# A graph network on one Trainium2 core: spreading rows in three bf16 parts instead of f32, with one table of places instead of two

## The chip, the cores and the metric

The kernel runs on 1 core of one Trainium2 chip. The metric is device time in microseconds (us) of one launch; lower is better. A "profiled execution" is one launch recorded instruction by instruction. Five engines work side by side, each through its own instructions in order, and wait for each other by semaphores: PE (TensorE, matrix products, with its weight loads shown apart as PEld), DVE (VectorE), ACT (ScalarE), POOL (GpSimd) and SP (SyncE, which here issues transfers).

## What is computed

There are N = 32768 nodes with rows of D = 256 numbers, and E = 524288 edges (`src`, `dst`), sorted by `dst`. Layer 0 is attention inside blocks of 128 nodes; layer 1 is a gated graph layer. Cut to what matters:

```python
h = relu(layernorm(x))
x = x + attention(h)                     # 256 blocks of 128 nodes, 8 heads of 32
h1 = relu(layernorm(x))
h = batchnorm(h1)
a_in  = segment_sum((h @ W_in  + b_in )[src] * iw[:, None], dst)
a_out = segment_sum((h @ W_out + b_out)[dst] * ow[:, None], src)
x = x + gate(concat(a_in, a_out), h)     # sigmoid and tanh gates
```

The sums are linear, so the kernel sums rows of `h1` first and multiplies by the weights afterwards. For `a_out` each edge needs the row `h1[dst]`, scaled by `ow`, and the results are to be added by `src`, in which the edges are not sorted.

## The kernel before

**Stages.** First the edges are counted and tables are made (to about 1035 us of the span). Then comes **spreading**, with the attention woven into it (1035 to 8983 us). It takes the edges in their `dst` order, builds for each one a message, which is its `h1[dst]` row times `ow`, and writes it to a place in HBM (`msg_d`) that groups the messages by blocks of `src`. Then the sums are made for both directions (8990 to about 15360 us), and the gates last.

**An item of spreading** is up to 128 edges whose `dst` lie in one block of 128 nodes. There are 4352 items in three phases, and a **round** is CI = 64 items. The functions `turns`, `fetch`, `spread_lanes`, `select`, `rank`, `product`, `place`, `scale` and `scatter` write the order out by hand under `manual_schedule`: turn t does step s of item t minus the lag of s, so each engine's instructions stand in the order of the turns, and within a turn in the order of the tuple `steps` (the product stands ahead of the place there).

- `fetch` (lag 0): SP loads the 128 rows of the block from `h1_d` into `hb`, 128 KB.
- `spread_lanes` (lag 4, every fourth item) and `select` (lag 6): PE spreads each edge's lane over the partitions (L1064), and DVE makes from it a 0/1 matrix `selT` in f32 (L1069) for four items at once. For each item DVE makes `oh`, a 0/1 matrix in bf16 that tells each edge's block of `src` among NB = 256 (L1071).
- `rank` (lag 8, PE, L1079) and `place` (lag 8, DVE, L1099): the table `R` in PSUM, 128 x 256 in f32, holds for each edge of the item and each block of `src` how many messages that block already has. `rank` adds products of `oh` to it, in bf16; `place` reads for each edge the one number that belongs to its block. There are **two tables**, and item i uses `R[i % 2]`. For each item three products are added to its table: all edges of item i-1 (`ones_b`), the rest of item i-2 (`triu`) and the earlier edges of item i (`tri`).
- `product` (lag 8, PE, L1075): `selT` times `hb` in f32 gives each edge its row (`mp`, two buffers). Each is two MATMUL records in the profile.
- `scale` (lag 9, ACT, L1091): times `ow`, into `msg`. `scatter` (lag 9, POOL, L1108): four indirect transfers at every fourth item, 128 messages each.

`rank` for item i+2 writes the table that `place` of item i reads, so it waits for that; `rank` for item i+1 does not.

**The attention** of one group of 512 nodes is a list of steps by turn (`group`): each is put with `@at(t)` into the turns of one round, after the turn's steps of spreading. 63 of the 64 groups lie in rounds of spreading, one in each; group 0 runs alone ahead. For each of a group's four blocks it makes scores (L837), their maxima (DVE, L845), the exponentials (ACT, L851), transposes (PE, L857), the products with V (L873), the output projection (L895), `x1g` (DVE, L899) and `h1g` (ACT, L922). Block b starts at turn B = 17 + 11 b. At turn B + 19 of the last block SP writes `h1g` to `h1_d`, from which later rounds fetch. Rounds stand in loop bodies of four (`UG`), and some of one.

**What sets the order** around the change is this hand-written list alone, on PE, DVE, ACT and SP; POOL follows its semaphores.

Of the kernel before, what the change touches and what calls it, by code (L numbers as in the profile page):

```python
# [23 lines left out]
KC = D // P  # L24
HC = H // KC
GB = 4
# [122 lines left out]
BF16 = mybir.dt.bfloat16  # L149
NB = 256  # L150
T1 = 128
# [348 lines left out]
def gnn_kernel(ctx, tc, x, src, dst, edge_attr, edge_type, w_in_e, w_out_e,  # L500
               Wq, bq, Wk, bk, Wv, bv, Wo, bo, gate_table, We, be,
               gamma, beta, W_in, b_in, W_out, b_out, W_x2i, b_x2i, W_h2h, out):
    nc = tc.nc
    N = x.shape[0]
# [4 lines left out]
    dram = ctx.enter_context(tc.tile_pool(name="dram", bufs=1, space=DRAM))  # L509


    cn = {}
# [30 lines left out]
    x1_d = dram.tile([N, D], F32, name="x1_d")  # L543
    h1T_d = dram.tile([D, N], F32, name="h1T_d")
    h1_d = dram.tile([N, D], F32, name="h1_d")
    rec_d = dram.tile([E + T2, 4], F32, name="rec_d")
    ends = [sum(PH[:k + 1]) for k in range(len(PH))]
    assert ends[-1] == E
# [11 lines left out]

    x1_g = x1_d.rearrange("(g b p) d -> g p b d", b=GB, p=P)
    h1_g = h1_d.rearrange("(g b p) d -> g p b d", b=GB, p=P)
    h1T_g = h1T_d.rearrange("(c p) (g n) -> g p c n", p=P, n=GN)


# [3 lines left out]
    soff = [before_each(nc, cpool, cn, t, f"src_off{k}") for k, t in enumerate(scnt)]  # L569
# [11 lines left out]
    for k, (lo, hi) in enumerate(edges):  # L581
        t = target_counts(nc, cpool, dcnt, doff, lo, hi, f"dcnt{k}")
        w0, node, r = item_tables(tc, cpool, cn, f"p{k}", t, lo, T1, CI, 0, NC1[k], hi, [("row", tab1_d[k][0:NC1[k]])])
# [55 lines left out]
    with tc.tile_pool(name="ld", bufs=1) as lp:  # L639
# [4 lines left out]
        for k in range(K):  # L644
            n, node = NC1[k], itp[k][1]
# [5 lines left out]
            r = lp.tile([CI, n], F32, name="r")  # L651
# [9 lines left out]
        g = lp.tile([P, 1], F32, name="g")  # L661
        nc.vector.tensor_copy(g, lead)
        for k in range(K):
            left = lp.tile([P, 1], F32, name="left")
            nc.vector.tensor_scalar(left, g, -1.0, float(NG), op0=ALU.mult, op1=ALU.add)
            at = lambda i: slice(i * K + k, i * K + k + 1)
# [20 lines left out]
    with ExitStack() as c1:  # L687
# [25 lines left out]
        xg, xb, x1g, h1g = (ap.tile([P, GB, D], F32, name=n) for n in ("xg", "xb", "x1g", "h1g"))  # L713
        hT, qT, h1T = (ap.tile([P, KC, GN], F32, name=n) for n in ("hT", "qT", "h1T"))
        nmr = ap.tile([P, GB], F32, name="nmr")

        mv, rstd = ([ap.tile([P, GB] + w, F32, name=f"{n}{i}") for i in range(2)] for n, w in (("mv", [2]), ("rstd", [])))

        def group(g, bias=None):
# [3 lines left out]
            def at(t):  # L723
                def put(f):
                    todo.setdefault(t, []).append(f)
                return put
# [100 lines left out]
            for b in range(GB):  # L827
# [89 lines left out]
                for n, u in enumerate(range(bs.start, bs.stop)):  # L917
                    h = {}

                    @at(B + 18 + n)  # L920
                    def _(u=u):
                        nc.scalar.activation(h1g[:, u], x1g[:, u], AF.Relu, bias=nmr[:, u:u + 1], scale=rstd[1][:, u:u + 1])  # L922

                    @at(B + 19 + n)
                    def _(u=u, h=h):
                        h["tp"] = transposed("pt" if u == 1 else "sc", h1g[:, u])

                    @at(B + 20 + n)
                    def _(u=u, h=h):
                        nc.scalar.copy(h1T[:, :, u * P:(u + 1) * P], h["tp"])  # L930
# [4 lines left out]

            @at(B + 19)
            def _():
                nc.sync.dma_start(h1_g[g], h1g)

            @at(B + 21)  # L940
            def _():
# [27 lines left out]
        ip = c1.enter_context(tc.tile_pool(name="p_i", bufs=NM))  # L969
        hp = c1.enter_context(tc.tile_pool(name="p_h", bufs=10))  # L970
        bp = c1.enter_context(tc.tile_pool(name="p_b", bufs=1, space=PSUM))
        pp = c1.enter_context(tc.tile_pool(name="p_ps", bufs=2, space=PSUM))
        p1 = c1.enter_context(tc.tile_pool(name="p_p1", bufs=1, space=PSUM))
        zm = fp.tile([P, T3 // P, MW], F32, name="zmsg")
        nc.vector.memset(zm, 0.0)
        nc.vector.memset(zm[:, :, FW:FW + 1], -1.0e6)
        eno = fp.tile([CI, T1], F32, name="eno")
        nc.gpsimd.iota(eno, pattern=[[1, T1]], base=0, channel_multiplier=0, allow_small_or_imprecise_dtypes=True)
        R = [p1.tile([P, NB], F32, name=f"R{i}") for i in range(2)]
        win = fp.tile([CI, T1 * 4], F32, name="win")  # L980
        wix = fp.tile([CI, 1], I32, name="wix")
        rown = fp.tile([1, CI], I32, name="rown")
# [9 lines left out]
        def spread(k, lo, hi):  # L992
# [6 lines left out]

            w0_1, node_1 = itp[k]  # L1000
            nc.scalar.dma_start(msg_d[k][hi - lo:hi - lo + T3].rearrange("(p e) w -> p e w", p=P), zm)
            for r in R:
                nc.tensor.matmul(r, cn["row0"], soff[k], start=True, stop=False, skip_group_check=True)

            def derive(c):

# [47 lines left out]
            def fetch(i, q, c, turn):  # L1054
                if q % 4 == 0:
                    c["at"] = numbers(c["row"][:, q:q + 4], [N - P] * 4)
                hb = turn["hb", i] = hp.tile([P, D], F32, name="hb")
                nc.sync.dma_start(hb, h1_d[ds(c["at"][q % 4], P)])

            def spread_lanes(i, q, c, turn):  # L1060
                if q % 4 == 0:
# [3 lines left out]

            def select(i, q, c, turn):
                if q % 4 == 0:
                    sel = turn["sel", i // 4] = sp.tile([P, 4, T1], F32, name="selT")
                    nc.vector.tensor_scalar(sel, turn["bc"], cn["lane"], None, op0=ALU.is_equal)  # L1069
                oh = turn["oh", i] = op.tile([P, NB], BF16, name="oh")  # L1070
                nc.vector.tensor_scalar(oh, cn["iota1"], c["ed"][:, 0, q:q + 1], None, op0=ALU.is_equal)  # L1071

            def product(i, q, c, turn):
                mp = turn["mp", i] = pp.tile([P, D], F32, name="mp")
                nc.tensor.matmul(mp, turn["sel", i // 4][:, q % 4], turn.pop(("hb", i)), start=True, stop=True)  # L1075

            def add(what, of, to, turn):
                oh = turn["oh", of]
                nc.tensor.matmul(R[to % 2], cn[what], oh, start=False, stop=False, skip_group_check=True)  # L1079

            def rank(i, q, c, turn):

                if i:
                    add("ones_b", i - 1, i, turn)
                if i > 1:
                    add("triu", i - 2, i, turn)
                add("tri", i, i, turn)

            def scale(i, q, c, turn):
                msg = msgs[i // 4 % NM]  # L1090
# [4 lines left out]
            def place(i, q, c, turn):  # L1095
                if q % 4 == 0:
                    c["pf"] = ip.tile([P, 4], F32, name="pf")
                jk = sp.tile([P, NB], F32, name="jk")
                nc.vector.scalar_tensor_tensor(jk, cn["iota1"], c["ed"][:, 0, q:q + 1], R[i % 2], op0=ALU.is_equal,  # L1099
                                               op1=ALU.mult, accum_out=c["pf"][:, q % 4:q % 4 + 1])  # L1100
                if q % 4 == 3:
                    c["pi"] = ip.tile([P, 4], I32, name="pi")
                    nc.vector.tensor_add(c["pi"], c["pf"], c["ed"][:, 3, q - 3:q + 1])
# [8 lines left out]
                        tc.add_to_no_dep_group(f"places{k}", s.ins)  # L1112


            steps = ((0, fetch), (4, spread_lanes), (6, select), (8, rank), (8, product), (8, place), (9, scale), (9, scatter))

            def turns(begin_at, end, nr, groups):

                with tc.For_i(begin_at, end, nr, hint_engines=ENGINES) as it:
                    cs, turn, todo, n = [], {}, {}, nr * CI  # L1120
                    last = steps[-1][0]
                    with tc.manual_schedule(engines=IN_ORDER):
                        for t in range(n + last):
                            r, q = divmod(t, CI)
                            if r < nr:
                                after = ds((it + (r + 1)).with_bounds(min_val=0, max_val=NC1[k]), 1)
                                if q == 0:
                                    cs.append({})
                                    begin(cs[r])
                                    if groups is not None:  # L1130
                                        for u, fs in group((it + groups + r).with_bounds(min_val=0, max_val=NG - 1)).items():
                                            assert u < CI + last
                                            todo.setdefault(t + u, []).extend(fs)
                                if q == 10:
                                    window(after)
                                if q == 24:
                                    more = derive(after)
                                if q >= 24:
                                    next(more, None)
                            for lag, step in steps:  # L1140
                                i = t - lag
                                if 0 <= i < n:
                                    step(i, i % CI, cs[i // CI], turn)
                            for f in todo.get(t, ()):
                                f()
                        add("ones_b", n - 1, n, turn)
                        add("triu", n - 2, n, turn)
                        add("triu", n - 1, n - 1, turn)

            window(slice(0, 1))  # L1150
            for _ in derive(slice(0, 1)):
# [272 lines left out]
```

## Time and profile before

| | |
|---|---|
| median of 11 runs | 17505.98 us (17489.43 to 17527.19) |
| profiled execution: its time, its span | 17473.85 us, 17472.0 us |
| mean granted TensorE clock | 0.913 |
| busy share of the span: PE, DVE, ACT, POOL | 81%, 58%, 38%, 53% |
| spreading with attention, 1100 to 8507 us: PE, DVE, ACT, POOL busy | 6174, 5115, 3607, 4145 of 7407 us |
| one round with attention, 2192.9 to 2305.0 us: the same | 98.1, 82.3, 58.2, 66.3 of 112.1 us |
| one round without attention, 8602 to 8700 us: the same | 59.7, 57.0, 32.3, 64.2 of 98.0 us |

The profiled execution is 32 us below the median of the runs. "Busy" for PE counts a matmul from its start to its modelled end; matmuls follow one another before the earlier one has ended, so the distance from start to start is what one costs. In a timeline, the first column is the start in us, the second the duration; `out<-in` are the tiles, and `[1.70 <-PE R L1079]` says that the engine sat idle for 1.70 us before and what it waited for. Line numbers are those of the kernel before.

### The profile page before, as it was taken

To read this page: it belongs to the slowest core of one execution; us is meant where nothing else is said; L and a number is where in the kernel's file an instruction comes from. 1 tells how busy PE (TensorE), PEld (TensorE's weight loads), DVE (VectorE), ACT (ScalarE), POOL (GpSimd) and SP (SyncE) were. 2 spreads that over 40 slices of the span, in tenths; PEclk is the share of its full clock that TensorE was granted. 3 is DMA by queue.
4 is the path that set the end of the run, shared out by engine and by line. 5 is a ranking of instruction groups with operands and counts; after the bars stand their busy time and mean duration, and the time that the engine had idled before them with its cause. 6 is when DMAs were issued, how large, how long until landed. Compare 5 with 4: busy or idle time off the path is not lost. (4 is left out here: it accounts for less than half of the span.)

```text
span 17472.0 us, 292322 instructions
## 1 busy us (share of the span) xinstructions
PE 14096.4 (81%) x71746; PEld 10263.3 (59%) x71746; DVE 10064.5 (58%) x33799; ACT 6700.4 (38%) x16865; POOL 9294.8 (53%) x9307
## 2 busy tenths in 40 slices
PE   2078888888888888888769889888888888888989
PEld 2045655555555555555457777777777777643433
DVE  8767667666766667667655555555555445422222
ACT  0034444444444444444334444444444444310000
POOL 0045555555555555555567667666666666621222
PEclk6589999999999899999889999999999999999999
DMA  1035555445555445555558888788878888843332
GB/s 63 10 123 169 163 164 166 158 154 163 168 159 162 158 134 164 160 162 163 165 174 241 229 232 236 220 227 223 231 218 228 220 225 230 195 126 106 115 115 90
DMA packets 1829631, 2975.49 MB, mean 170 GB/s; under 512 B 299499, under 2 KB 1288136, under 8 KB 1827671
## 3 DMA queue, kind: packets, MB, share of 16 engines
q1 hardware_dynamic: 1169398, 1550.90, 30.4%
q0 software_dynamic: 430768, 1160.40, 22.9%
q10 hardware_dynamic: 227888, 246.51, 4.6%
q8 instruction: 582, 9.54, 0.2%
q14 instruction: 995, 8.14, 0.2%
HBM read 2123.63 MB, written 1248.64 MB: 193 GB/s over the span
## 5 line engine op out<-in xcount | busy, mean ns | idle before, releaser
L1108 POOL DMA_INDIRECT msg_d<-msg,pi x4352 | 4288.3, 985 | 3018.6 <-ACT msg L1091 1069.2
L1230 POOL DMA_INDIRECT rows<-h_d,ixc x3584 | 3403.9, 950 | 1560.1 <-PE ps_i L1244 449.3
L1099 DVE SCALAR_TENSOR_TENSOR jk<-iota,edc,R 128x256 f32<-128x256 bf16 x4352 | 2076.1, 477 | 1896.2 <-PE R L1079 1867.2
L1091 ACT ACTIVATE msg<-mp,edc 128x256 f32<-128x256 f32 x4352 | 2056.8, 477 | 2738.4 <-PE mp L1075 2699.5
L1265 ACT ACTIVATE selo<-lane_row,sl 128x128 f32<-128x128 f32 x5040 | 1664.0, 391 | 3623.8 <-DVE sl L1262 2966.6
L1272 PE MATMUL ps_o<-m,selo 128*128 128x257 f32 x10080 | 2596.9, 395 | 336.4 <-ACT selo L1266 332.3
L1244 PE MATMUL ps_i<-rows,sel 128*128 128x257 f32 x8960 | 2511.8, 399 | 370.0 <-DVE acc L1248 295.0
L1075 PE MATMUL mp<-hb,selT 128*128 128x256 f32 x8704 | 2760.3, 401 | 8.1 <-ACT msg L1091 7.1
L1272 PEld LDWEIGHTS ps_o<-m,selo 128*128 128x128 f32 x10080 | 1876.7, 196 | 671.8 <-ACT selo L1266 261.5
L1244 PEld LDWEIGHTS ps_i<-rows,sel 128*128 128x128 f32 x8960 | 1572.5, 199 | 626.3 <-DVE acc L1248 402.2
L1237 DVE TENSOR_SCALAR sel<-lane_row,ed 128x128 f32<-128x128 f32 x4480 | 1394.1, 359 | 561.8 <-PE idle L1245 506.2
L1075 PEld LDWEIGHTS mp<-hb,selT 128*128 128x128 f32 x8704 | 1399.7, 202 | 82.6 <-ACT msg L1091 13.8
L1071 DVE TENSOR_SCALAR oh<-iota,edc 128x256 bf16<-128x256 bf16 x4352 | 1415.6, 325 | 4.1
L1079 PE MATMUL R<-oh,ones_b 128*128 128x256 bf16 x4352 | 1245.9, 286 | 119.5 <-DVE jk L1099 111.3
L1276 DVE SCALAR_TENSOR_TENSOR acc<-acc,blk,ps_o 128x257 f32<-128x257 f32 x1680 | 806.0, 480 | 826.7 <-PE ps_o L1272 630.6
L1079 PE MATMUL R<-oh,tri 128*128 128x256 bf16 x4352 | 1238.1, 284 | 0.0
L1079 PE MATMUL R<-oh,triu 128*128 128x256 bf16 x4352 | 1231.2, 283 | 0.0
L1248 DVE SCALAR_TENSOR_TENSOR acc<-acc,blk,ps_i 128x257 f32<-128x257 f32 x2240 | 1071.1, 478 | 252.1 <-DMA sin_d<-acc 137.4
L1262 DVE TENSOR_SCALAR sl<-m,blk 128x3 f32<-128x3 f32 x1680 | 426.8, 254 | 1363.6 <-DMA m<-msg_d 1354.1
L1230 POOL DMA_INDIRECT rows<-h_d,ixh x896 | 849.9, 948 | 385.2 <-issue 135.2
L1266 ACT ACTIVATE selo<-selo,one 128x384 f32<-128x384 f32 x1680 | 1031.4, 614 | 52.2
L1245 PE MATMUL idle<-lane_row,sel 128*128 128x128 f32 x4480 | 852.2, 279 | 148.3 <-DVE sel L1237 141.2
(366 smaller groups left out, 20238.5 us busy)
## 6 DMA issues: line engine op xcount, KB each, us to landing
m<-msg_d SPq DMA_DIRECT2D x1680, 396.0 KB
hb<-h_d SPq DMA_DIRECT2D x4352, 128.0 KB
sin_d<-acc SPq DMA_DIRECT2D x2240, 128.5 KB
sout_d<-acc SPq DMA_DIRECT2D x1680, 128.5 KB
msg_d<-msg,pi POOLq DMA_INDIRECT x4352
more<-sout_d ACTq DMA_DIRECT2D x128, 514.0 KB
rows<-h_d,ixc POOLq DMA_INDIRECT x3584
a<-sin_d ACTq DMA_DIRECT2D x64, 514.0 KB
```

Of the source, the lines that this page charges most:

```text
L1071: nc.vector.tensor_scalar(oh, cn["iota1"], c["ed"][:, 0, q:q + 1], None, op0=ALU.is_equal)
L1075: nc.tensor.matmul(mp, turn["sel", i // 4][:, q % 4], turn.pop(("hb", i)), start=True, stop=True)
L1079: nc.tensor.matmul(R[to % 2], cn[what], oh, start=False, stop=False, skip_group_check=True)
L1091: nc.scalar.activation(msg[:, q % 4, 0:D], turn.pop(("mp", i)), AF.Copy, scale=c["ed"][:, 1, q:q + 1])
L1099: nc.vector.scalar_tensor_tensor(jk, cn["iota1"], c["ed"][:, 0, q:q + 1], R[i % 2], op0=ALU.is_equal, op1=ALU.mult, accum_out=c["pf"][:, q ...
L1108: s = nc.gpsimd.indirect_dma_start(out=msg_d[k][:], out_offset=bass.IndirectOffsetOnAxis(ap=c["pi"][:, j:j + 1], axis=0), in_=msgs[i // 4 ...
L1230: nc.gpsimd.indirect_dma_start(out=rows[(2 * i + r) % NR][:, 0:D], out_offset=None, in_=h1_d[:], in_offset=bass.IndirectOffsetOnAxis(ap=(i ...
L1237: nc.vector.tensor_scalar(sel[:, r], cn["lane_row"], c["ed"][:, 0, r, i:i + 1], c["ed"][:, 1, r, i:i + 1], op0=ALU.is_equal, op1=ALU.mult)
L1244: nc.tensor.matmul(ps, sel[:, r], rows[(2 * i + r) % NR], start=(r == 0), stop=(r == 1))
L1248: nc.vector.scalar_tensor_tensor(acc[0][i % NA], acc[0][(i - 1) % NA], c["blk"][:, 0, i:i + 1], c.pop(("t_ps", i)), op0=ALU.mult, op1=ALU.add)
L1265: nc.scalar.activation(sel[:, r], cn["lane_row"], AF.Abs, bias=sl[:, r:r + 1])
L1272: nc.tensor.matmul(ps, sel[:, r], m[:, r, 0:FW], start=(r == 0), stop=(r == T3 // P - 1))
```

## The change

`group` now writes the rows of `h1` a second time, to `h1s_d`, as three bf16 parts whose sum is the row: the row rounded to bf16, what is left rounded again, and what is left then. These are two ACT copies and two DVE subtractions for each block of 128 nodes. The write of `h1s` (768 KB for each group, at turn B + 22) takes SP; the write of `h1g` moves from SP to ACT. `fetch` loads the three parts (192 KB for each item). `selT` becomes bf16, and `product` is three bf16 matmuls into one `mp`, which gets a third buffer. `rank` keeps one table `R` and adds two products for each item, the rest of item i-1 and the earlier edges of item i. `place` stands ahead of `product` in the tuple.

```diff
+    h1s_d = dram.tile([N, 3, D], BF16, name="h1s_d")
...
+        h1s = ap.tile([P, GB, 3, D], BF16, name="h1s")
+        rest = ap.tile([P, GB, D], F32, name="rest")
...
+                    @at(B + 19 + n)
+                    def _(u=u):
+                        nc.scalar.copy(h1s[:, u, 0], h1g[:, u])
+
+                    @at(B + 20 + n)
+                    def _(u=u):
+                        nc.vector.tensor_sub(rest[:, u], h1g[:, u], h1s[:, u, 0])
+                        nc.scalar.copy(h1s[:, u, 1], rest[:, u])
+
+                    @at(B + 21 + n)
+                    def _(u=u):
+                        nc.vector.tensor_sub(h1s[:, u, 2], rest[:, u], h1s[:, u, 1])
...
             @at(B + 19)
             def _():
-                nc.sync.dma_start(h1_g[g], h1g)
+                nc.scalar.dma_start(h1_g[g], h1g)
+
+            @at(B + 22)
+            def _():
+                nc.sync.dma_start(h1s_g[g], h1s)
...
-        pp = c1.enter_context(tc.tile_pool(name="p_ps", bufs=2, space=PSUM))
+        pp = c1.enter_context(tc.tile_pool(name="p_ps", bufs=3, space=PSUM))
...
-        R = [p1.tile([P, NB], F32, name=f"R{i}") for i in range(2)]
+        R = p1.tile([P, NB], F32, name="R")
...
-                hb = turn["hb", i] = hp.tile([P, D], F32, name="hb")
-                nc.sync.dma_start(hb, h1_d[ds(c["at"][q % 4], P)])
+                hb = turn["hb", i] = hp.tile([P, 3, D], BF16, name="hb")
+                nc.sync.dma_start(hb, h1s_d[ds(c["at"][q % 4], P)])
...
-                    sel = turn["sel", i // 4] = sp.tile([P, 4, T1], F32, name="selT")
+                    sel = turn["sel", i // 4] = sp.tile([P, 4, T1], BF16, name="selT")
...
                 mp = turn["mp", i] = pp.tile([P, D], F32, name="mp")
-                nc.tensor.matmul(mp, turn["sel", i // 4][:, q % 4], turn.pop(("hb", i)), start=True, stop=True)
-
-            def add(what, of, to, turn):
-                oh = turn["oh", of]
-                nc.tensor.matmul(R[to % 2], cn[what], oh, start=False, stop=False, skip_group_check=True)
+                hb = turn.pop(("hb", i))
+                for part in range(3):
+                    nc.tensor.matmul(mp, turn["sel", i // 4][:, q % 4], hb[:, part], start=(part == 0), stop=(part == 2))
+
+            def add(what, of, turn):
+                nc.tensor.matmul(R, cn[what], turn["oh", of], start=False, stop=False, skip_group_check=True)
 
             def rank(i, q, c, turn):
 
                 if i:
-                    add("ones_b", i - 1, i, turn)
-                if i > 1:
-                    add("triu", i - 2, i, turn)
-                add("tri", i, i, turn)
+                    add("triu", i - 1, turn)
+                add("tri", i, turn)
...
-                nc.vector.scalar_tensor_tensor(jk, cn["iota1"], c["ed"][:, 0, q:q + 1], R[i % 2], op0=ALU.is_equal,
+                nc.vector.scalar_tensor_tensor(jk, cn["iota1"], c["ed"][:, 0, q:q + 1], R, op0=ALU.is_equal,
...
-            steps = ((0, fetch), (4, spread_lanes), (6, select), (8, rank), (8, product), (8, place), (9, scale), (9, scatter))
+            steps = ((0, fetch), (4, spread_lanes), (6, select), (8, rank), (8, place), (8, product), (9, scale), (9, scatter))
...
-                        add("ones_b", n - 1, n, turn)
-                        add("triu", n - 2, n, turn)
-                        add("triu", n - 1, n - 1, turn)
+                        add("triu", n - 1, turn)
```

More of the change, by code (lines that the diff above doesn't have):

```diff
@@ L562, in gnn_kernel @@
     h1_g = h1_d.rearrange("(g b p) d -> g p b d", b=GB, p=P)
+    h1s_g = h1s_d.rearrange("(g b p) s d -> g p b s d", b=GB, p=P)
     h1T_g = h1T_d.rearrange("(c p) (g n) -> g p c n", p=P, n=GN)
@@ L1001, in spread @@
             nc.scalar.dma_start(msg_d[k][hi - lo:hi - lo + T3].rearrange("(p e) w -> p e w", p=P), zm)
-            for r in R:
-                nc.tensor.matmul(r, cn["row0"], soff[k], start=True, stop=False, skip_group_check=True)
+            nc.tensor.matmul(R, cn["row0"], soff[k], start=True, stop=False, skip_group_check=True)
             def derive(c):
```

## The prediction

> **What bounds the kernel now.** I read the page's slices first, then busy time by stage, then the waits of spreading, and last the timeline of a few turns, because the change trades work on one engine for an order between two. The slices are 437 us each, in tenths:
>
> ```profile
> PE   2078888888888888888769889888888888888989
> ...
> DVE  8767667666766667667655555555555445422222
> ```
>
> Slices 4 to 20 are spreading. PE is busiest but never full there, and DVE is close behind. By stage (all spreading with attention, one round with attention, one without; columns are PE, PEld, DVE, ACT, POOL busy us, granted clock, DMA share, GB/s):
>
> ```profile
> 1100.00:8507.00 7407.00, 6174.24 (x35713) 4337.28 (x35711) 5115.37 (x18694) 3607.36 (x9306) 4144.78 (x4125) 0.92 0.50 161
> ...
> 2192.90:2305.00 112.10, 98.12 (x574) 68.85 (x572) 82.33 (x300) 58.21 (x151) 66.28 (x66) 0.94 0.54 172
> ...
> 8602.00:8700.00 98.00, 59.67 (x388) 42.48 (x388) 57.03 (x243) 32.30 (x82) 64.22 (x65) 0.80 0.53 172
> ```
>
> In a round with attention neither PE nor DVE fills the 112.1 us; together they do, by turns. In the round without attention nothing but POOL does: a scatter starts every 1.29 us, so 64 take 82.6 us, and the rest is start and drain. Who waits in the woven stage, and what ended DVE's waits ahead of `place` in the one round:
>
> ```profile
> ACT msg L1091 <- PE mp L1075: 2398.3, 2256, 5.1
> DVE jk L1099 <- PE R L1079: 1828.7, 1933, 4.7
> ...
> PEld pt L857 <- ACT pr L851: 262.9, 126, 2.3
> ```
> ```profile
>   PE R L1079: 27.8, 30
> ```
>
> DVE waits for the table in 30 of 64 items: there PE paces. In the other 34 DVE comes to `place` late, after its attention work, and PE runs ahead. Four turns of both, items 36 to 39 of one round:
>
> ```profile
> 2966.18 0.28 PE L1079 MATMUL R<-oh,ones_b 128*128 128x256 bf16 x1
> ...
> 2966.72 0.48 DVE L1099 SCALAR_TENSOR_TENSOR jk<-iota,edc,R 128x256 f32<-128x256 bf16 x1 [1.70 <-PE R L1079]
> ...
> 2966.95 0.27 PE L1079 MATMUL R<-oh,ones_b 128*128 128x256 bf16 x1
> ...
> 2967.13 0.42 DVE L899 TENSOR_TENSOR x1g<-mm,xb 128x256 f32<-128x256 f32 x1
> ...
> 2967.72 0.27 PE L1079 MATMUL R<-oh,ones_b 128*128 128x256 bf16 x1
> ...
> 2968.14 0.66 DVE L845 TENSOR_REDUCE nm<-sc 128x4 f32<-128x512 f32 x1
> ...
> 2968.91 0.47 DVE L1099 SCALAR_TENSOR_TENSOR jk<-iota,edc,R 128x256 f32<-128x256 bf16 x1
> ...
> 2969.31 0.69 DVE L865 COPY PT<-pt 128x512 f32<-128x512 f32 x1
> ...
> 2970.15 0.41 PE L857 MATMUL pt<-ident,pr 128*128 128x128 f32 x2 [1.50 <-ACT pr L851]
> ...
> 2970.39 0.27 PE L1079 MATMUL R<-oh,ones_b 128*128 128x256 bf16 x1
> ...
> 2970.77 0.47 DVE L1099 SCALAR_TENSOR_TENSOR jk<-iota,edc,R 128x256 f32<-128x256 bf16 x1
> ```
>
> `rank` of items 36, 37, 38, 39 starts at 2966.18, 2966.95, 2967.72, 2970.39; their places at 2966.72, 2968.91, 2970.77. PE begins rank 38 1.2 us before place 37 begins. Two tables allow that; one does not.
>
> **The change, part by part.** All per round with attention (63 of them), then times 63.
>
> *PE work.* From rank to rank with nothing between is 0.77 us (2966.95 to 2967.72): three bf16 products at 0.11, and the f32 product in two records for the remaining 0.43. The new item is two and three bf16 products, 5 x 0.11 = 0.55. That is 0.21 us less for each item, 13.7 a round, 930 us of PE time in all. The weight loads (L1079, three an item today) lie beside the products now; I take it that the three loads of `selT` do too. In the 34 items where DVE paces nothing of it shows; in the 30 where PE does, at most 30 x 0.21 = 6.4 us a round.
>
> *The order between rank and place.* New chain of each item: rank start to place start 0.42 (0.11, then 0.27 of the second product, then 0.04; today with three 0.54), place 0.48, about 0.07 to PE: 0.97 us an item at least, and rank i+1 behind place i. I walked items 30 to 41 of this round (one attention block) through the timeline with today's durations, each engine in its order. From item 36, with its rank left at 2966.18: place 36 ends 2967.08, rank 37 goes to 2967.15 (+0.20). DVE's L899 to L845 and `oh` then run 0.12 earlier than today, place 37 ends 2969.27, so rank 38 goes to 2969.34 (+1.62). The transposes of L857 wait for the copy of L865 anyway, so they start at 2970.03, before today's. Place 38 follows L865, the `selT` of four items (0.74) and `oh`: 2970.65 to 2971.13, rank 39 at 2971.20 (+0.81). Rank 40 comes at 2972.30 (+0.50), rank 41 at 2973.27 (+0.71). Over the whole block, with the 0.21 taken off each item, rank 41 is 0.97 us later than today, which is 17.11 us after rank 30. Three such blocks in a round: **+3.0**; the last, shorter stretch I take at half a block, **+0.5**. The eleven items at the round's start with 512-column products, where PE paces clearly, get the full saving: **-2.4**.
>
> *The parts of h1.* Eight DVE subtractions; `x1g` (L899, 128x256 f32) takes 0.42, about 0.34 in a row with others, so 2.7 us. They fall at turns 59 to 62 and 70 to 71, where DVE is mostly the later one: two thirds on the path, **+1.8**. Eight ACT copies, between L889 (0.38, from PSUM) and L922 (0.62, from SBUF): 4 us beside 58 of 112 busy, at zero, hidden by PE and DVE; the copies wait for a subtraction of the same turn, and behind them stand `scale` and the exponentials. The third `mp` lets PE go on then. Without that cover it is the whole 4.
>
> *Queues.* The write of `h1s` (768 KB) waits on SP for the last subtraction and for all fetches under way, and the next fetches stand behind it. Today, in one round, fetching stops at 2179.96, the 512 KB write goes at 2186.84 and the next fetch at 2190.43, a hole of 10.5 us; a fetch is used eight turns later, 14 us. With 1.5 times the bytes the hole is 12.3: still covered, at zero; past 14 it is paid in full. At a body's end POOL is last: in the body that ends near 2420 the write goes at 2410.66, POOL's last scatter ends at 2419.92 and fetching resumes at 2425.61. A write three turns later that takes 5.4 us is inside that. The write of `h1g` costs ACT 0.4 (L942's issue, 0.38), at zero. Bytes: 64 KB more for 4352 fetches and 768 KB for 64 groups, 335 MB over 7950 us, 42 GB/s on 161; the sums stage runs at 225. Zero. The rounds without attention stay at POOL's 1.29, since 0.97 is below it. All later stages read `h1_d` as before: zero.
>
> *The clock.* Where PE is busy 98.12 of 112.1, the granted clock is 0.94; at 59.67 of 98.0 it is 0.80. Taking 13.7 us out of about 115 makes PE 73% busy, which lies at 0.86 on the line between the two rows. That is 8% of PE's pace: 9 us a round if PE paced all of it, nothing where DVE does. The row without attention holds a long start and drain, so the woven row is nearer; I take **+1.5** and keep 0 to 9.
>
> [...]
>
> *Sum:* 3.0 + 0.5 - 2.4 + 1.8 + 1.5 = **+4.4 us a round**, times 63 = **+277 us**, on the profiled execution's 17473.85: 17,751. That execution is 32 us under the median of the runs; on the median, 17,505.98 + 277, it is **17,783 us**, 1.6% slower.
>
> **The rivals.**
>
> *PE paces, the wait is absorbed (faster).* If rank's later start falls into waits that PE has anyway, as at L857 above (1.50 idle), the saving is 30 x 0.21 less the subtractions: -6.4 + 1.8 = -4.6 a round, -290 us: 17,216. For it: DVE's 1828.7 us of waiting for R, and 0.12 less from rank to place. Against it: the walk, in which +1.62 came down only to +0.71, because PE-heavy turns follow DVE-heavy ones, and one table turns the sum of both into the sum of the larger.
>
> *The lag is paid in full (much slower).* In the round of the walk 26 of 64 places end after the next rank has started; the largest of each run, added up, are 16 us. With 1.8 and 5 for the clock, less 2.4, that is +20 a round, +1,290: 18,796. Against it: L857 shows that part of each lag meets a wait.
>
> *They cancel.* -2.4 and -1.0 against 3.0 and 0.5 with subtractions hidden: within 35 us of 17,506.
>
> *The bf16 parts save nothing.* If three loads of the same weights do not hide, each product costs up to 3 x (0.11 + 0.10) = 0.63 instead of 0.43. The load of L1079 takes 0.10 and shows no cost in the 0.11 steps, so I give it little: with +0.2 in 30 items, +6 more on the sum, +655 in all: 18,161.
>
> **How the numbers follow.** The sum's own case 0.62, with own range +1 to +9 a round (the clock from 0 to 9, the stretches walked only in part): 17,570 to 18,075. PE paces: 0.22. Cancel: 0.06. Paid in full: 0.06. Parts save nothing: 0.04. What a measurement of this kernel can tell from no change is about 0.2%, 35 us. The range for 8 in 10 reaches to the upper half of the faster case and to the rival with the unhidden loads: 17,300 to 18,150. Faster over 0.2%: 0.23, the first rival and a rest of the sum's low end. Within: 0.06. Slower: 0.71.
>
> **What would show it.** In the new profile: the line of the product with 13,056 matmuls that follow at 0.11; the table with two products an item; DVE waiting for R in more items but for less in each; PE waiting for DVE's `jk`, which today is near nothing, for several us in each round; PE less busy and clock under 0.92 from 1100 to 8507; a round of about 116 us; unchanged rounds without attention and unchanged later stages. Wrong would be: rounds near 107 with little waiting for `jk` (the first rival), a round far above 120 (the lag, or the clock), or PE waiting for `hb` (the queue).

## The result, and the profile after

| | before | after |
|---|---|---|
| median of the runs | 17,503.89 us (31 runs) | 17,931.14 us (17,902.98 to 17,942.44, 8 runs) |
| ratio, 95% interval | | 1.0242 [1.0233, 1.0251] |
| profiled execution: time, span | 17,473.85, 17,472.0 us | 17,956.11, 17,954.4 us |
| mean granted clock | 0.913 | 0.881 |

The change costs 2.4%. The forecast was 17,783 us, in a range of 17,300 to 18,150. The direction was right; the size was 148 us short. The two profiled executions lie further apart than the medians, 482 us against 427, so the loss that is taken apart below from the profiles is some 55 us larger than the loss in the table.

All of it is lost in spreading. From the first `place` to the last it takes 7,919.0 us before and 8,403.6 us after, +484.6; the two profiled executions differ by 482.3. In the slices of the new page the loss is seen as a lower clock over the first half; the last line is the clock of the page before:

```profile
PE   2077777777777768777758888888888888889888
...
PEclk6578888888888888888889999999999999999999
```
```profile
PEclk6589999999999899999889999999999999999999
```

By stage, the same stretch of the span as before, 1100 to 8507 us (PE, PEld, DVE, ACT, POOL busy, granted clock, DMA share, GB/s):

```profile
1100.00:8507.00 7407.00, 5678.22 (x33679) 3852.45 (x33678) 4998.42 (x18102) 3557.87 (x9246) 3938.04 (x3886) 0.84 0.61 191
```

PE did 496 us less here (6174.24 to 5678.22) and POOL got less far, 3,886 instructions against 4,125. No engine became fuller: DVE, ACT and POOL all fell too. So no engine became the bound; waiting grew. Who waits, 1100 to 8950 us (us in all, times, longest):

```profile
ACT msg L1111 <- PE mp L1098: 2329.1, 2007, 4.7
DVE jk L1119 <- PE R L1101: 2106.0, 2147, 4.2
...
PE R L1101 <- DVE jk L1119: 928.5, 1098, 4.0
...
ACT h1s L940 <- DVE rest L939: 376.1, 249, 2.7
...
PEld pt L743 <- ACT PT L867: 188.1, 62, 3.1
```

The same view of before:

```profile
DVE jk L1099 <- PE R L1079: 1846.6, 1961, 4.7
...
PE R L1079 <- DVE jk L1099: 111.3, 73, 3.3
...
PEld pt L739 <- ACT PT L863: 40.7, 63, 1.4
```

Three things are new. PE waits for `place` before it may change the one table: 111 us became 929. (What such waits cost is another question: e3 below has 1,020 us of them and is faster than after.) ACT waits 376 us for the first subtraction: 249 waits, one for nearly every block of the 63 groups. And PE's transposes of L743 wait longer for ACT's copy of `PT`, although no step of the change touches that copy.

To see where in a round the time goes, I took the distances from `place` to `place` in the 28 rounds that have attention and no end of a loop body near, and added them in three stretches. The busy times and the clock are those of the same stretches. The other columns are the first four experiments below, which ran on a chip where before takes 17,520 us.

| mean of 28 rounds, us | before | after | e1 two tables | e2 one table alone | e3 no parts made | e4 filler |
|---|---|---|---|---|---|---|
| whole round | 112.95 | 121.49 | 116.8 | 113.6 | 114.9 | 121.3 |
| items 0 to 47 | 82.86 | 86.75 | 81.10 | 84.41 | 84.95 | 86.90 |
| their clock | 0.97 | 0.91 | 0.96 | 0.98 | 0.94 | 0.99 |
| items 48 to 55 | 13.35 | 18.57 | 19.58 | 12.76 | 14.35 | 18.12 |
| their DVE, ACT busy | 8.7, 9.3 | 10.8, 11.1 | 10.8, 11.0 | 8.6, 9.3 | 8.7, 9.1 | 10.7, 11.2 |
| their clock | 0.88 | 0.62 | 0.64 | 1.00 | 0.72 | 0.78 |
| items 56 to 63 | 16.74 | 16.17 | 16.13 | 16.46 | 15.60 | 16.31 |

Eight items, 48 to 55, take 5.2 of the 8.5 us that a round lost. These are the turns in which the parts of `h1` are made. The windows of one round show the same stretch, before and then after:

```profile
3097.80:3111.10 13.30, 11.13 (x71) 8.32 (x72) 8.76 (x38) 9.31 (x24) 5.98 (x7) 0.87 0.37 122
```
```profile
3251.60:3269.90 18.30, 14.85 (x75) 10.71 (x75) 10.81 (x43) 11.10 (x30) 7.32 (x9) 0.63 0.41 124
```

DVE does 2.05 us more and ACT 1.79 us more, but the stretch is 5.0 us longer, and neither is full: DVE is busy 10.8 of 18.3 us, where it was 8.8 of 13.3. A turn of it, in the timeline of after (start, duration, engine):

```profile
3255.90 0.27 PE L1101 MATMUL R<-oh,triu 128*128 128x256 bf16 x1
...
3256.01 0.27 PE L1101 MATMUL R<-oh,tri 128*128 128x256 bf16 x1
...
3256.32 0.48 DVE L1119 SCALAR_TENSOR_TENSOR jk<-iota,edc,R 128x256 f32<-128x256 bf16 x1 [1.02 <-PE R L1101]
...
3256.92 0.42 DVE L939 TENSOR_TENSOR rest<-h1g,h1s 128x256 f32<-128x256 f32 x1
...
3257.37 0.40 ACT L940 CAST h1s<-rest 128x256 bf16<-128x256 f32 x1 [0.77 <-DVE rest L939]
...
3258.76 0.57 ACT L867 COPY PT<-pt 128x512 f32<-128x512 f32 x1
...
3259.38 0.69 PE L743 MATMUL pt<-ident,h1g 128*128 128x128 f32 x2 [2.77 <-ACT PT L867]
...
3260.53 0.40 PE L1101 MATMUL R<-oh,triu 128*128 128x256 bf16 x1
...
3260.72 0.42 PE L1101 MATMUL R<-oh,tri 128*128 128x256 bf16 x1
...
3261.18 0.48 DVE L1119 SCALAR_TENSOR_TENSOR jk<-iota,edc,R 128x256 f32<-128x256 bf16 x1 [3.65 <-PE R L1101]
...
3261.93 0.42 DVE L939 TENSOR_TENSOR rest<-h1g,h1s 128x256 f32<-128x256 f32 x1
...
3262.38 0.41 ACT L940 CAST h1s<-rest 128x256 bf16<-128x256 f32 x1 [2.68 <-DVE rest L939]
```

Read it as a ring. `place` (DVE) ends at 3256.80, and the subtraction stands behind it. ACT has waited 0.77 us for the subtraction of this same turn. Behind that cast on ACT stand the copy of `h1T`, the next cast, `h1g`, and the copy of `PT` (3258.76 to 3259.33). PE's transposes wait for `PT`, 2.77 us idle, and `rank` of the next item stands behind the transposes in PE's order. So the next `place` starts at 3261.18, 4.86 us after this one, and DVE has waited 3.65 of them. Each turn passes through all three engines one after the other, once for each cast.

### The profile page after: what moved, and what is told of

The parts are those of the page before. It is cut to its first block, busy times and chain, and to the rows that moved or that the text cites. A ratio compares the mean times of both kernels' runs of the same rounds, so it can differ in the third digit from the quotient of the medians.

```text
span 17954.4 us, 289429 instructions
## 1 busy us (share of the span) xinstructions
PE 13900.9 (77%) x71740; PEld 9969.0 (56%) x71740; DVE 10255.1 (57%) x34311; ACT 6870.6 (38%) x17377; POOL 9344.4 (52%) x9307
## 5 line engine op out<-in xcount | busy, mean ns | idle before, releaser
L1098 PE MATMUL mp<-hb,selT 128*128 128x256 bf16 x13056 | 2478.0, 305 | 3.8 <-DMA hb<-h1s_d 3.3
L1101 PE MATMUL R<-oh,triu 128*128 128x256 bf16 x4352 | 1308.2, 301 | 1029.3 <-DVE jk L1119 1016.1
L1098 PEld LDWEIGHTS <-selT 128*128 128x128 bf16 x13056 | 1422.4, 109 | 311.4 <-issue 5.6
L1092 DVE TENSOR_SCALAR oh<-iota,edc 128x256 bf16<-128x256 bf16 x4352 | 1367.2, 314 | 4.1
L1101 PEld LDWEIGHTS <-tri 128*128 128x128 bf16 x4352 | 448.8, 103 | 1619.1 <-issue 1582.9
L1101 PE MATMUL R<-oh,tri 128*128 128x256 bf16 x4352 | 1327.4, 305 | 0.0
```

The source lines that it names most:

```text
L1098: nc.tensor.matmul(mp, turn["sel", i // 4][:, q % 4], hb[:, part], start=(part == 0), stop=(part == 2))
L1101: nc.tensor.matmul(R, cn[what], turn["oh", of], start=False, stop=False, skip_group_check=True)
```

## The experiments

"After" is the changed kernel. The theory at the start: two costs, the order of one table and the making of the parts, with the lower clock as a consequence. The rivals: the clock itself costs the time; the larger transfers do.

### e1: two tables again

```diff
-        R = p1.tile([P, NB], F32, name="R")
+        R = [p1.tile([P, NB], F32, name=f"R{i}") for i in range(2)]
...
-        pp = c1.enter_context(tc.tile_pool(name="p_ps", bufs=3, space=PSUM))
+        pp = c1.enter_context(tc.tile_pool(name="p_ps", bufs=2, space=PSUM))
...
-                    add("triu", i - 1, turn)
-                add("tri", i, turn)
+                    add("ones_b", i - 1, i, turn)
+                if i > 1:
+                    add("triu", i - 2, i, turn)
+                add("tri", i, i, turn)
...
```

The third `mp` is given up for the second table: `mp` has two buffers here.

> The changed kernel with its tables undone: two tables R in turn, three products an item for them, and two mp buffers as before (the bank of the third goes to the second table). Rows stay in three bf16 parts. If the wait of rank for the place just ahead is the main cost (theory A), PE's waits for jk go from 928 us to about the 109 of before, and the time from 17,931 to about 17,580 (63 rounds less 3.5 for the order and about 2 of clock). If the lower clock is the main cost (B), PE's work rises only by 0.11 of the missing 0.21 us an item and about half of the loss comes back: about 17,720. If making or moving the parts is (C), it stays above 17,850.

Measured: 17,736.78 us, 1.0128 [1.0111, 1.0145], 194 us under after. The time is near the 17,720 of theory B, but what is seen inside is theory A: PE's waits for `jk` fall from 928.5 to 140.2 us, while the clock of 1100 to 8950 us rises only from 0.84 to 0.86. A's 17,580 isn't reached, since the cost of the parts stays. In the table above, items 0 to 47 fall from 86.75 to 81.10 us, below before's 82.86: there the bf16 products do save, 1.8 us, as long as the places alternate between tables. Items 48 to 55 stay long (19.58). So on top of bf16 rows one table costs 5.65 us in items 0 to 47 and 4.7 over the whole of such a round, and the trouble of the parts doesn't come from it.

### e2: one table alone

```diff
-        R = [p1.tile([P, NB], F32, name=f"R{i}") for i in range(2)]
+        R = p1.tile([P, NB], F32, name="R")
...
-                    add("ones_b", i - 1, i, turn)
-                if i > 1:
-                    add("triu", i - 2, i, turn)
-                add("tri", i, i, turn)
+                    add("triu", i - 1, turn)
+                add("tri", i, turn)
...
```

This and e10 start from the kernel before; all others from after.

> The kernel before with one table alone: two products an item for R, rows and product in f32, two mp buffers. A: the wait alone costs about what it costs in the change, 3.5 to 7 us a round, less up to 0.11 in the items that PE paces: 17,504 rises to about 17,750, with several hundred us of PE waiting for jk. B: half of the missing PE work, so half of the loss, 17,700, and a clock near 0.88 from 1100 us to the end of spreading. C: no loss, 17,500 or below.

Measured: 17,569.15 us, 1.0028 [1.0016, 1.0041]. That is below what either theory A (17,750) or B (17,700) expected. PE waits 747.6 us for `jk` here, and the loss, net of the table product that each item saves, is 49 us. The clock of 1100 to 8950 us is 0.93, not the 0.88 of B. The same table costs 49 us here and 194 us in e1's comparison. With f32 rows items 0 to 47 lose 1.55 us, and items 48 to 55 gain 0.6 at a full clock of 1.00. The parts of the change don't add: 0.28% for the table and 1.28% for the bf16 rows make 1.56%, and together they cost 2.42%.

### e3: no parts made

```diff
-        rest = ap.tile([P, GB, D], F32, name="rest")
+        nc.vector.memset(h1s, 0.0)
...
-                        nc.scalar.copy(h1s[:, u, 0], h1g[:, u])
...
-                        nc.vector.tensor_sub(rest[:, u], h1g[:, u], h1s[:, u, 0])
-                        nc.scalar.copy(h1s[:, u, 1], rest[:, u])
...
-                        nc.vector.tensor_sub(h1s[:, u, 2], rest[:, u], h1s[:, u, 1])
```

> The changed kernel without making the parts: h1s is zeroed once, the two ACT copies and two DVE subtractions of each block of 128 nodes are left out (the rows that are spread are zeros), and its write and its fetches stay. A and B: 1.8 us a round less, 17,931 falls to about 17,820. C, with the parts the main cost: to 17,600 or below.

Measured: 17,662.78 us, 1.0087 [1.007, 1.0104], 268 us under after. This is 4.3 us for each of the 63 rounds, and the largest single cost; the time lies between the 17,820 of A and B and the 17,600 of C. All bytes are still written and fetched (they are zeros), so the cost comes from the eight subtractions and eight casts of a round, on DVE and ACT. Items 48 to 55 take 14.35 us; all but 1.0 of their 5.2 us is gone. PE's waits for `jk` are 1,019.6 us here, more than in after, so they aren't what the 268 us consist of.

### e4: a filler that brings the clock back

```diff
+                for _ in range(2):
+                    nc.tensor.matmul(mp, turn["sel", i // 4][:, q % 4], hb[:, 0], start=True, stop=True)
```

> The changed kernel with two more bf16 products an item into mp, which the true ones then overwrite: PE's work an item is as before the change (0.76 us), the order is that of the change. B: the granted clock in spreading goes from 0.84 back to about 0.92 and the time falls, to 17,750 or below. A: the clock may rise, but the items that PE paces pay 0.22 each, 6 us a round, so the time stays or rises, 17,900 to 18,250.

Measured: 18,043.09 us, 1.0304 [1.0287, 1.0321], 112 us over after. The clock came back, as the stretch 1100 to 8950 us shows, first after, then this one:

```profile
1100.00:8950.00 7850.00, 6000.65 (x35627) 4071.28 (x35625) 5283.60 (x19144) 3764.77 (x9786) 4165.18 (x4112) 0.84 0.60 190
```
```profile
1100.00:8950.00 7850.00, 6277.47 (x43130) 4561.34 (x43130) 5231.07 (x18950) 3733.01 (x9679) 4105.66 (x4070) 0.91 0.60 189
```

The 28 rounds of the table take 121.3 us with the filler and 121.5 without, though 128 products were put into each, 14 us at the 0.11 us that one takes. The sum of the round hides two opposite effects. Items 30 to 41, the block that the prediction walked, take 21.26 us in after, at a clock of 0.81, and 19.02 here, at 1.00. Items 12 to 47 together take 66.65 us instead of 67.67, with 72 products more. The order is the same and PE has only got more to do, so what was gained can hardly come from anything but the clock: here the low clock is a cost. At the round's start the filler costs as much: items 0 to 11 go from 19.08 to 20.25 us. In items 48 to 55 the clock rises from 0.62 to 0.78 for a gain of 0.45 us, with 16 products more. Over the whole kernel a clock that is brought back with this work brings no time back. The two profiled executions differ by 82 us, and that lies in the 35 other rounds with attention, which take 4,632 us together instead of 4,548.

### e8, e8b: the second cast one turn later

What e3 leaves open is whether the parts cost their work or the waiting in the ring. This kernel keeps every operation and moves two of them by one turn each, so that ACT's cast takes a subtraction of the turn before.

```diff
                     @at(B + 20 + n)
                     def _(u=u):
                         nc.vector.tensor_sub(rest[:, u], h1g[:, u], h1s[:, u, 0])
+
+                    @at(B + 21 + n)
+                    def _(u=u):
                         nc.scalar.copy(h1s[:, u, 1], rest[:, u])
 
-                    @at(B + 21 + n)
+                    @at(B + 22 + n)
                     def _(u=u):
                         nc.vector.tensor_sub(h1s[:, u, 2], rest[:, u], h1s[:, u, 1])
```

> The changed kernel with the second ACT copy of each part put one turn later (B + 21 + n) and the second subtraction behind it (B + 22 + n); the work is the same. In the trace of the change ACT's copy waits for the subtraction of the same turn, and the transposes of PE wait for what stands behind it on ACT. If this ring is what the parts cost (theory D), most of the 268 us that leaving them out gave comes back: 17,931 falls to 17,700 to 17,780, and items 48 to 55 of a round from 18.6 us to about 15. If it is the work itself (E: 8 subtractions and 8 copies, 6 us of engine time a round), nothing changes: 17,900 to 17,950.

> The changed kernel, with the second copy to bf16 one turn later than the subtraction it waits for, and the second subtraction one turn later than that. No operation is added or taken away. Ring theory (the cost of making the parts is that ScalarE waits for a subtraction of the same turn, and the transposes and the next table product wait behind it): items 48 to 55 of a round come down from 18.6 us to about 15, 3 to 4 us a round, so 17,700 to 17,780. Rival, the work itself (eight subtractions on VectorE and sixteen copies on ScalarE cost what they cost wherever they stand): 17,900 to 17,950, as the changed kernel.

The runs from here on were made on two chips on which before itself takes 19,601.53 us (e5, e7, e8, e9) and 19,512.86 us (e5b, e8b, e9b, e10), so only ratios to before and differences within one chip are used. The ratios don't carry over either: the change cost 2.4% where it was first measured, and e7 and e5, which are close to it, cost 1.2 to 1.5% here. After itself didn't run there; e7 and e5 below, which differ from it by one buffer and by the bytes fetched, stand in for it.

Measured: 19,768.69 us, 1.0094 [1.0061, 1.0126], and 19,622.25 us, 1.0054 [1.0033, 1.0075]. It is 102 us under e7 and 126 under e5 on the one chip, 128 under e5b on the other. Waits of 1100 to 8950 us in e5b, and then in e8b:

```profile
ACT h1s L940 <- DVE rest L939: 368.1, 219, 4.7
PEld pt L743 <- ACT PT L867: 191.6, 58, 3.7
```
```profile
PEld pt L743 <- ACT PT L867: 101.7, 58, 2.1
...
ACT h1s L943 <- DVE rest L939: 5.5, 13, 0.5
```

ACT's wait for the subtraction is gone (368.1 to 5.5), and PE's wait for `PT` behind it is nearly halved. Items 48 to 55 take 15.96 us against 18.35, while DVE and ACT are busy there as long as before (10.7 and 10.8 us against 10.7 and 10.7): it was waiting, not work. On the other chip the same items take 16.32 us in e8 against 18.55 in e7. The clock of these items rises with it, from 0.62 to 0.72, and a part of the gain may be the clock's; in e4 a larger rise, with 16 products more to carry, gave 0.45 us. The ring theory is borne out in its place; in its size it is short, 2.4 us in these items instead of 3 to 4, and 1.4 us over the whole round, since items 0 to 47 took 0.8 longer. So of the 268 us of the parts some 100 to 130 are the ring, with the reservation that these are two chips' numbers, and the rest is not split further.

### e9, e9b: late cast and two tables

The edits of e1 and e8 together, two buffers for `mp` among them.

> The late copy and two tables together (two mp buffers). D: as much less than the two-table run as the late copy gains on the change, 17,737 to about 17,540, the time of before (17,504 to 17,520). E: 17,700 to 17,740.

> [...] Ring theory: the two gains add up, the 194 us of the two tables on top of the late copy, about 17,540. Rival, the work itself: 17,700 to 17,740, as with two tables alone. If the two gains are one and the same (either way out of the wait frees the same turns), 17,650 to 17,740 as well, with the late copy alone faster.

Measured: 19,854.93 us, 1.0128 [1.0097, 1.0159], and 19,698.15 us, 1.0094 [1.0068, 1.0119]: 86 and 76 us over the late cast alone, on both chips. The gains don't add up; with the late cast the second table loses. Part of the loss can be placed: items 48 to 55 take 17.14 us in e9b against 15.96 in e8b, and 17.60 in e9 against 16.32 in e8, much as they take 19.58 in e1 against 18.57 in after. What is missing is the gain of the second table in items 0 to 47: 97.52 us in e9b, 97.26 in e8b. These items are 9 us and more longer on these chips than on the first, in every version that was profiled there, so the missing gain may belong to the chips; e1 alone wasn't run on them. This stays open.

### e5, e5b: two thirds of the bytes

```diff
-                hb = turn["hb", i] = hp.tile([P, 3, D], BF16, name="hb")
-                nc.sync.dma_start(hb, h1s_d[ds(c["at"][q % 4], P)])
+                hb = turn["hb", i] = hp.tile([P, 2, D], BF16, name="hb")
+                nc.sync.dma_start(hb, h1s_d[ds(c["at"][q % 4], P), 0:2])
...
-                    nc.tensor.matmul(mp, turn["sel", i // 4][:, q % 4], hb[:, part], start=(part == 0), stop=(part == 2))
+                    nc.tensor.matmul(mp, turn["sel", i // 4][:, q % 4], hb[:, part % 2], start=(part == 0), stop=(part == 2))
```

> The changed kernel with fetches of 128 KB, as before the change: only the first two parts are loaded, and the third product takes the first part again (its sums are other ones). If the bytes cost something (F), the time falls by 50 us or more under 17,931; if they are hidden, as was predicted, it stays within 30 us of it.

> The changed kernel, but each fetch of rows brings two of the three parts (128 KB instead of 192 KB), and the third product of an item multiplies the first part again: TensorE's work is the same, the bytes fetched are those of before. The output then lacks the third part. If the bytes are hidden: within 30 us of 17,931. If the half more bytes cost: 50 us or more lower.

Measured: 19,895.15 us, 1.0154 [1.0124, 1.0184], and 19,750.7 us, 1.0122 [1.0095, 1.015]. The expected absolute times don't apply on these chips. But with the bytes of before it is no faster than e7, which fetches all three parts (19,870.65); the third buffer, the other difference to e7, does nothing (see e7). So the larger fetches are hidden. PE's wait for a fetched row on the page of after says the same:

```profile
L1098 PE MATMUL mp<-hb,selT 128*128 128x256 bf16 x13056 | 2478.0, 305 | 3.8 <-DMA hb<-h1s_d 3.3
```

It is 3.3 us (the last number) in the whole execution; in e5b it is 0.7.

### e7: two buffers for the products

```diff
-        pp = c1.enter_context(tc.tile_pool(name="p_ps", bufs=3, space=PSUM))
+        pp = c1.enter_context(tc.tile_pool(name="p_ps", bufs=2, space=PSUM))
```

> The changed kernel with two mp buffers in place of three. If the third buffer carries part of the change (G), the time rises by 50 us or more above 17,931, since product then waits for scale of two items back, while ACT stands waiting for the subtractions; otherwise it stays within 30 us.

Measured: 19,870.65 us, 1.0141 [1.0109, 1.0174], 24 us under e5, which has three: well inside the intervals. The page of e7 shows why:

```profile
L1098 PE MATMUL mp<-hb,selT 128*128 128x256 bf16 x13056 | 2573.2, 314 | 4.0 <-DMA hb<-h1s_d 2.3
```

With two buffers PE sat idle ahead of its products for 4.0 us in the whole execution, 2.3 of them for a fetched row. That leaves at most 1.7 us of waiting for a free `mp`.

### e10: one table and a third buffer, rows in f32

The edit of e2, and:

```diff
-        pp = c1.enter_context(tc.tile_pool(name="p_ps", bufs=2, space=PSUM))
+        pp = c1.enter_context(tc.tile_pool(name="p_ps", bufs=3, space=PSUM))
```

> The kernel before with one table, two table products an item, rows left in f32, and the freed bank given to a third buffer for the products of the rows. With two buffers this was 17,569. If the third buffer lets TensorE go on where it waits for ScalarE's copy of a product, 17,450 to 17,520, under the kernel before; if the lag between place and rank is what counts, 17,560 to 17,580, as with two.

Measured: 19,705.39 us, 1.0088 [1.0059, 1.0116]. It was the candidate to beat before, and it doesn't. Its 0.9% can't be set against the 0.3% of e2, which ran on another chip. But e2's own page leaves a third buffer nothing to do: with two, PE sat idle ahead of the product for 0.4 us in the whole execution. No version of this study beats the kernel before.

## Why the prediction was right, and where its sum was off

**What bounds the kernel.** The reading that PE and DVE pace by turns, and that one table makes the sum of both into the sum of the larger, held. PE's wait for `jk` was predicted as "several us in each round"; it is 928.5 us over 63 rounds, 14.7 in each. DVE waits for R more often, as said, but not for less in each: 2106.0/2147 is 0.98 us, where it was 1846.6/1961 = 0.94. A round was to take about 116 us; the 28 rounds take 121.5.

**PE work.** The step from one bf16 product to the next is 0.109 us in the median of the trace after, against 0.218 for the f32 record: the price was right, and the rival in which the parts save nothing is out. The closest places (fifth percentile) follow each other at 0.95 us, before at 0.60; the forecast chain was 0.97. The saving of 2.4 us in the eleven items at the round's start did not come: items 0 to 11 fell by 0.56 (19.64 to 19.08), and by 0.9 even with two tables. That PE "paces clearly" there was read from the 512-column products and not from a walk.

**The order of one table.** The walk forecast +0.97 for its block with the saving of the products taken off, and +3.5 for all blocks. The block, from item 30 to 41, takes 18.02 us before and 21.26 after, in the mean of the 28 rounds: +3.24. Items 12 to 47 together lost 4.45 us (63.22 to 67.67). What the walk lacked is the clock: it moved today's durations about, and in after the clock of this block is 0.81, where it was 0.95. With a clock near full the block comes out near the walk's 18.99: 18.97 us in e2 (0.97) and 19.02 in e4 (1.00). So the order itself was priced about right in this block; the step that was too small is the clock's, which here adds some 2 us to eleven items, more than the 1.5 set aside for a whole round. That e2 and e4 agree with the walk to 0.05 us is luck in part, since neither has the walk's full saving on PE. Over items 0 to 47 one table costs 1.55 us with f32 rows (e2) and 5.65 with bf16 rows (e1 to after); how much of this difference is the clock outside of the walked block isn't shown.

**The parts of h1: the term that was mis-sized most.** The sum had 1.8 us, for the subtractions alone, with the ACT copies "at zero, hidden by PE and DVE". Undone, the parts give back 4.3 us a round (e3). The prediction named the queue: the copies wait for a subtraction of the same turn. But it put only `scale` and the exponentials behind them, and let the third `mp` carry PE over. What stands behind them too is the copy of `PT`; PE waits for that one, not for an `mp`, and a third buffer can't help (e7). The waiting itself is shown by e8: with the same work one turn later ACT's wait goes from 368 to 5.5 us and 100 to 130 us come back. What makes up the rest of the 268 isn't shown. The case that the prediction named, "Without that cover it is the whole 4", would have made this term 5.8 us, above the 4.3. The term was short by 2.5 us, times 63 = 157 us, and the whole forecast by 148. That the two agree is luck: the saving at the round's start (2.4 forecast, 0.56 measured) and the clock of the walked block were off in the same direction, the end of the round (items 56 to 63, -0.6) in the other, and the single experiments don't add up (e2).

**The clock.** Forecast 0.86 by the line between two rows, measured 0.84, though PE was busier than forecast, 77% instead of 73%. Its price over a whole round can't be read off; in the walked block it is some 2 us (e4). These are the rows of after for the turn shown above, in the columns used before:

```profile
3255.73:3259.14 3.41, 0.88 (x8) 0.55 (x6) 1.18 (x5) 2.64 (x8) 0.00 (x0) 1.00 0.55 155
3259.15:3269.38 10.23, 10.00 (x50) 7.67 (x50) 5.85 (x24) 4.26 (x13) 4.15 (x4) 0.50 0.30 91
```

A stretch of 3.41 us in which PE was busy for 0.88 us stood at full clock, and the 10.23 us behind it at half, though PE was busy for 10.00 of them.

**Queues, bytes, the rest.** Set to zero, and zero they were, as far as shown: rounds without attention take 97.2 to 97.4 us after the first, before 97.1 to 98.0; the 21 rounds with a body's end lost 5.1 us (130.3 to 135.4), less than the 8.5 of the 28; fewer bytes gave nothing (e5). From the last `place` to the end of the span it is 8,518 us before and 8,514 after.

**The rivals.** PE paces, and the wait is absorbed: out, though its saving exists where two tables remain (e1, items 0 to 47). The lag in full, +20 a round: out, at +8.5. (The 16 us that it was built on come to 14.6 in the trace of that round, or 15.4 with the 0.07 to PE each time; it is out either way.) Cancelling is nearest to e2 alone, which has no bf16 rows.

## What to carry to other kernels

A small step that is added to an engine with spare time is free only if nothing that another engine waits for stands behind it in the queue; list what is queued behind it, and ask of each who waits, before writing zero. Here it was the copy of `PT`, and PE's wait for it went from 40.7 to 188.1 us. A cast that needs a result of another engine from the same turn ties the two together; one turn later, with the same work, that wait fell from 368 to 5.5 us. Waiting that an engine does is not yet a loss: e3 has more waits for the one table than after, 1,020 us against 929, and is 268 us faster. And whether filling PE's holes for the sake of the clock pays depends on the stretch: in e4 it took 2.2 us off one block and put 1.2 us on another, and nothing was left of it in the round. A buffer that lets one engine run ahead of another should be given up only after looking at what faster work would do with it: the single table cost 0.3% with f32 rows and 1.1% once the products were cheaper.

## What the hardware showed that I had not expected

PE's granted clock in after was 0.62 over the items 48 to 55, in which PE was busy 14.7 of 18.6 us by its modelled ends. In the clock records of the profiled executions of before and after, from 1100 to 8950 us, the clock is 1.0 or 0.5, and each value lasts for a whole number of stretches of 3.41 us. Counted are the stretches of that length at full clock, by the share of them in which PE was busy. Of those under 40% all were followed by half clock (91 of 91 before, 148 of 148 after), of those with 60% or more none (0 of 1,582 and 0 of 1,154), and between the two 74 of 215 and 147 of 284. That is a count in two traces; what sets the clock they don't show.

Chips differ, or the times at which they were used; the runs don't tell these apart. On the two chips of the later runs before takes 19,602 and 19,513 us, 12% and 11% more. The instructions last as long there: in e5b a scatter takes 0.99 us and a `place` 0.48, as in after. But holes appear between them. In the rounds without attention scatters start 1.29 us apart in the median in both; the ninetieth percentile is 1.29 in after and 4.9 in e5b. In the slices of the next stage (the 23rd to the 34th) 186 to 202 GB/s are moved there, 220 to 234 in after. What makes the holes stays open.
